# First attention of a four-stage block: the softmax sums of a head group are formed by VectorE additions and one late product with ones

## The chip, the cores and the metric

One core of one Trainium2 chip runs the whole program. The metric is device time in microseconds (us), the median of repeated executions. Engines are named as in the profile: PE is TensorE (PEld its weight loads), DVE is VectorE, ACT is ScalarE, POOL is GpSimd, SP issues most DMAs.

## The reference, cut to what matters

Four residual stages run one after the other on x of shape 4 x 512 x 512: an attention, a feed-forward with ternary weights, a selective scan, and a second attention with a mixture of experts. Only the first attention is touched by the change:

```
q, k, v = heads of (x @ W_qkv.T), 16 heads of 32; q and k rotated, then RMS-normalized
scores = (q . k) / sqrt(32), causal mask
attn   = softmax(scores);   out = (attn @ v) @ W_o.T;   x = x + out
```

The kernel takes exp of the scores without subtracting a maximum, zeroes the masked part, multiplies the weights with v, and divides by the sum of the weights over keys.

## The kernel before, in words

Everything is float32 in this stage. The four batches b are taken one by one. `attend(b, between)` (line 332) works on transposed scores: keys lie on partitions, queries on the free axis. Heads go in four groups g of four heads (HG = 4), keys in four tiles j of 128. Because of the mask, tile j needs only the queries from 128*j on, so it is w = 512 - 128*j wide: 512, 384, 256, 128. The 16 pairs (g, j) are the steps m = 4g + j.

- `scores(g, j)` (line 340) makes four products on PE, one for each head, each with 32 rows (line 346), into two PSUM pairs `sc`; ACT takes exp in two halves into the SBUF tile `pt` (line 351); POOL zeroes the masked corner in the first 128 columns (affine_select, line 352).
- `weigh(g, j)` (line 357) makes eight products on PE (line 364): four with v into the PSUM bank `av`, four with a matrix of ones into the bank `sm`. Each uses 32 columns of the array, one column strip for each head. After j = 3, DVE takes the reciprocal of `sm` (line 372) and multiplies `av` with it (line 373) into `oT`.
- A float32 product shows as two records in the profile, so a set of four products is "x8".

In step m the order on PE is: scores of m, then the parts listed in `between[m]`, then weigh of m - 1. The parts are the projections of the next batch (`project`, line 268: 12 of them, in m = 0 and m = 5 to 15), the output projection of the previous batch (`back`, line 324, in m = 1 to 4), the scaling of q and k (`scale_heads`, line 295, on DVE, in m = 9 and 14), transposes (`turn_heads`, line 317, m = 12 and 13), and small pieces of preparing the ternary weights (`next_job`, line 208: a DMA of `q_w`, then ACT or DVE work). Batch 0 has no `back`, so its steps 1 to 4 have no part; batch 3 has no projections, so its steps 0 and 5 to 16 have no PE part but a tiny one. After the steps come two `turn_heads` and, for the first two batches, the norm of batch b + 2 and `turn_in` (line 262: DVE makes a `row`, two buffers; PE transposes it).

PE's order is the program's, written out by hand (`manual_schedule`, line 387). The order on DVE, ACT and POOL is chosen at build time by a planner that has its own durations; on the chip each of these queues is strictly in that order. A later operation that is ready does not pass one that waits.

Buffers that matter: `pt` has two buffers, so exp of step m writes the one that step m - 2 used. PSUM has eight banks: two pairs for `sc` and four single banks (`bank`, line 67) shared by `av`, `sm`, the projections `pq` and `y`, and the transposes `tp`. `r` has two buffers. The pool `wbig` (line 148) has two buffers of 24 KB a partition for wqkv, w1 and later w3.

Of the kernel before, what the change touches and what calls it, by code (L numbers as in the profile page):

```python
# [11 lines left out]
F32 = mybir.dt.float32  # L12
I32 = mybir.dt.int32
F32R = mybir.dt.float32r
AF = mybir.ActivationFunctionType
ALU = mybir.AluOpType
# [3 lines left out]
P = 128  # L20
B, T, C = 4, 512, 512
NT = T // P
NK = C // P
H, D = 16, 32
NG = H * D // P
HG = P // D
HID = 1365
# [19 lines left out]
def block_kernel(ctx: ExitStack, tc: tile.TileContext, a: dict, out: bass.AP):  # L47
    nc = tc.nc
# [33 lines left out]
    ones = const.tile([P, P], F32, tag="ones", name="ones")  # L82
# [62 lines left out]


    first = ExitStack()
    wbig = first.enter_context(tc.tile_pool(name="wbig", bufs=2, side="right"))


    with tc.tile_pool(name="a_w", bufs=1) as aw, tc.tile_pool(name="a_1", bufs=1) as a1, tc.tile_pool(
        name="a_2", bufs=2
    ) as a2:
        wqkv = wbig.tile([P, NK, 3 * C], F32, tag="wbig", name="wqkv")
        src = by_rows(a["wqkvT"])
# [35 lines left out]
        HW = (HID + 1) // 2  # L191
        parts = {}

        def place(name):
            return wbig.tile([P, NK, HID], F32R, tag="wbig", name=name)

# [45 lines left out]
            scales[name] = ternary_scale(a1, parts[name], name)  # L244

        scales = {}
        w1 = place("w1")

# [66 lines left out]
        def turn_heads(b, t):  # L317
            flat = heads[b][:, t].rearrange("p h d -> p (h d)")
            for s in range(2):
                transpose_into(  # L320
                    turned_qk[b][:, s * NG : (s + 1) * NG, :], flat[:, s * C : (s + 1) * C], t * P
                )
# [9 lines left out]
        def attend(b, between):  # L332

            qkT, v = turned_qk[b], values[b]
            oT = outs[b] = a1.tile([P, NK, T], F32, tag="oT", name="oT")
            weights, sums = {}, {}

            def scores(g, j):  # L340
                w = T - j * P
                pt = weights[g, j] = a2.tile([P, HG, T], F32, tag="pt", name="pt")
                both = [pair("sc") for _ in range(2)]
                for i in range(HG):
                    rows = slice(i * D, (i + 1) * D)
                    nc.tensor.matmul(  # L346
                        both[i // 2][:, i % 2, :w], qkT[rows, NG + g, j * P : (j + 1) * P],
                        qkT[rows, g, j * P :], start=True, stop=True,
                    )
                for i, sc in enumerate(both):  # L350
                    nc.scalar.activation(pt[:, 2 * i : 2 * i + 2, :w], sc[:, :, :w], AF.Exp, scale=SCALE)  # L351
                nc.gpsimd.affine_select(  # L352
                    out=pt[:, :, 0:P], in_=pt[:, :, 0:P], compare_op=ALU.is_ge, fill=0.0,
                    base=0, pattern=[[0, HG], [1, P]], channel_multiplier=-1,
                )

            def weigh(g, j):
                if j == 0:
                    sums[g] = bank("av"), bank("sm")
                pt = weights.pop((g, j))  # L360
                for s, dst in enumerate(sums[g]):
                    for i in range(HG):
                        h = g * HG + i
                        nc.tensor.matmul(
                            dst[i * D : (i + 1) * D, j * P :],
                            ones[:, :D] if s else v[:, j, h * D : (h + 1) * D],
                            pt[:, i, : T - j * P], start=j == 0, stop=j == NT - 1,
                        )
                if j == NT - 1:
                    av, sm = sums.pop(g)  # L370
                    r = a2.tile([P, T], F32, tag="r", name="r")
                    nc.vector.reciprocal(r, sm)
                    nc.vector.tensor_tensor(oT[:, g, :], av, r, ALU.mult)

            steps = [(g, j) for g in range(NG) for j in range(NT)]
            for m in range(len(steps) + 1):
                if m < len(steps):
                    scores(*steps[m])
                for part in between.get(m, ()):
                    part()  # L380
                if m > 0:
                    weigh(*steps[m - 1])

        def do(f, *args):
            return lambda: f(*args)

        with tc.manual_schedule(engines={mybir.EngineType.PE}):

            norm(0, 2)
            for i in range(2):  # L390
                turn_in(0, i)
                for t in (2 * i, 2 * i + 1):
                    project(0, t, 0)
                    project(0, t, 1)
                scale_heads(0, i)
            for i in range(2):
                project(0, 2 * i, 2)
                project(0, 2 * i + 1, 2)
                turn_heads(0, 2 * i)
                turn_heads(0, 2 * i + 1)  # L400
            norm(1)
            turn_in(1, 0)
            turn_in(1, 1)
            w3 = None

            for n in range(2 * NK):
                measure("w1", n)
            at_step = {(0, 1 + 2 * n): n for n in range(2 * NK)}
            scale_at = {(1, 0): "w1", (2, 10): "w2", (3, 0): "w3"}
            for n in range(2 * NK):  # L410
                at_step[1, 1 + 2 * n] = len(jobs)
                quantize(lambda: w1, "w1", n)
                at_step[1, 2 + 2 * n] = len(jobs)
                measure_down(n)
            for n in range(2 * NK):
                if n + 2 * NK < NF:
                    at_step[2, 1 + 2 * n] = len(jobs)
                    measure_down(n + 2 * NK)
                at_step[2, 2 + 2 * n] = len(jobs)
                measure("w3", n)  # L420
            for n in range(2 * NK):
                at_step[3, 1 + 2 * n] = len(jobs)
                quantize(lambda: w3, "w3", n)
            fetch_piece()
            fetch_piece()
            w3 = None
            for b in range(B):
                between = {m: [] for m in range(18)}
                if b > 0:
                    for t in range(NT):  # L430
                        between[1 + t].append(do(back, b - 1, t))
                if b + 1 < B:
                    n = b + 1
                    order = [(0, 0), (0, 1), (1, 0), (1, 1), (0, 2), (2, 0), (2, 1), (1, 2)]
                    order += [(3, 0), (3, 1), (2, 2), (3, 2)]
                    for m, (t, s) in zip([0] + list(range(5, 16)), order):
                        between[m].append(do(project, n, t, s))
                    between[9].append(do(scale_heads, n, 0))
                    between[12].append(do(turn_heads, n, 0))
                    between[13].append(do(turn_heads, n, 1))  # L440
                    between[14].append(do(scale_heads, n, 1))

                for m in range(17):
                    if (b, m) in scale_at:
                        between[m].append(do(find_scale, scale_at[b, m]))
                    if (b, m) in at_step:
                        between[m].append(do(next_job, at_step[b, m]))
                if b == B - 1:
                    first_mv = const.tile([P, NT, 2], F32, tag="mv", name="mv")
                    for t in range(NT):  # L450
                        between[9].append(do(statistics, a1, xs[0], t, first_mv))
                attend(b, between)
                if b + 1 < B:
                    turn_heads(b + 1, 2)
                    turn_heads(b + 1, 3)
                if b + 2 < B:
                    norm(b + 2)
                    turn_in(b + 2, 0)
                    turn_in(b + 2, 1)
                if b + 2 == B:  # L460
                    w3 = place("w3")
            for t in range(NT):
                back(B - 1, t)

# [131 lines left out]
    with tc.tile_pool(name="b_s", bufs=1) as bs, tc.tile_pool(name="b_1", bufs=1) as b1, tc.tile_pool(  # L596
        name="b_2", bufs=2
# [78 lines left out]
        with tc.manual_schedule(engines={mybir.EngineType.PE}):  # L676
# [4 lines left out]
            for b in range(B):  # L681
                hT = high_low.pop(b)
                between = prepare(b - 1, bs, half_pair, 2) if b > 0 else iter(())
# [135 lines left out]
    with tc.tile_pool(name="c_f", bufs=2, reuse_waits="tile") as cf, tc.tile_pool(  # L819
        name="c_1", bufs=1  # L820
# [5 lines left out]
        steps = [(b, n, half) for b in range(B) for n in range(NS) for half in range(2)]  # L826
        loaded, scaled, decays, turned, states, weighed, sums = {}, {}, {}, {}, {}, {}, {}
# [72 lines left out]
        between = prepare(B - 1, cp, bank, 4)  # L900
# [127 lines left out]
    with tc.tile_pool(name="d_1", bufs=1) as d1, tc.tile_pool(name="d_2", bufs=2) as d2, tc.tile_pool(  # L1028
        name="d_3", bufs=3
# [65 lines left out]
        probs, turned_probs, sums, wides, inverses, averages, outs = {}, {}, {}, {}, {}, {}, {}  # L1095
# [79 lines left out]
        with tc.manual_schedule(engines={mybir.EngineType.PE}):  # L1175
# [5 lines left out]
            for m in range(n + 3):  # L1181
                b, at = divmod(m, each)
# [35 lines left out]
    with tc.tile_pool(name="e_1", bufs=1, reuse_waits="tile") as e1, tc.tile_pool(  # L1218
        name="e_2", bufs=2, reuse_waits="tile"
# [55 lines left out]
        total = e1.tile([P, NR], F32, tag="total", name="total")  # L1275
# [15 lines left out]
        place = e1.tile([P, NR, TT], F32, tag="place", name="place")  # L1291
# [247 lines left out]
```

## Time and profile before

| | |
|---|---|
| median of 3 runs | 1933.17 us (1933.12 to 1936.76) |
| profiled execution: its own time | 1941.33 us |
| its span on the core | 1939.6 us |
| mean granted TensorE clock | 0.967 |
| PE busy | 1764.7 us (91%) |
| DVE, ACT, POOL busy | 1143.7 (59%), 946.0 (49%), 580.8 (30%) |
| first attention, first to last score | 63.5 to 412.9 us |

A row of the group view reads: line, engine, operation, what it writes <- what it reads, shapes, count | busy us, mean ns of one | idle time of the engine just before, and what ended it. A row of the timeline reads: start, us, engine, line, operation, count [idle before <- releaser]. Busy times on PE are modelled and overlap a little at the ends; the distance between two starts is the better measure of what one set of products costs.

### The profile page before, as it was taken

To read this page: it belongs to the slowest core of one execution; us is meant where nothing else is said; L and a number is where in the kernel's file an instruction comes from. 1 tells how busy PE (TensorE), PEld (TensorE's weight loads), DVE (VectorE), ACT (ScalarE), POOL (GpSimd) and SP (SyncE) were. 2 spreads that over 40 slices of the span, in tenths; PEclk is the share of its full clock that TensorE was granted. 3 is DMA by queue.
4 is the path that set the end of the run, shared out by engine and by line. 5 is a ranking of instruction groups with operands and counts; after the bars stand their busy time and mean duration, and the time that the engine had idled before them with its cause. 6 is when DMAs were issued, how large, how long until landed. Compare 5 with 4: busy or idle time off the path is not lost. (4 is left out here: it accounts for less than half of the span.)

```text
span 1939.6 us, 26716 instructions
## 1 busy us (share of the span) xinstructions
PE 1764.7 (91%) x9970; PEld 1063.5 (55%) x9970; DVE 1143.7 (59%) x1849; ACT 946.0 (49%) x1945; POOL 580.8 (30%) x391
## 2 busy tenths in 40 slices
PE   7999999989999996977888788999999989999998
PEld 3433343437666664766776655555555554544544
DVE  6456435666454545898999985566574663422222
ACT  2433433332242434978999955556675662111111
POOL 2221212120202020966999850000001000144441
PEclk9999999999999998978999987999999999999999
DMA  7003200101000104115131100000001004645445
GB/s 246 8 1 94 75 1 1 44 25 53 1 34 12 44 1 146 40 60 168 53 101 53 50 14 1 1 1 23 1 23 33 23 2 145 223 88 92 87 83 140
DMA packets 67525, 111.09 MB, mean 57 GB/s; under 512 B 7627, under 2 KB 26443, under 8 KB 67349
## 3 DMA queue, kind: packets, MB, share of 16 engines
q1 hardware_dynamic: 58164, 88.02, 13.8%
q0 software_dynamic: 8656, 20.32, 5.8%
q8 instruction: 80, 1.31, 0.3%
q10 hardware_dynamic: 576, 1.05, 0.1%
q14 instruction: 49, 0.39, 0.1%
HBM read 81.18 MB, written 31.33 MB: 58 GB/s over the span
## 5 line engine op out<-in xcount | busy, mean ns | idle before, releaser
L875 POOL TENSOR_TENSOR hc<-h,cb 128x1024 f32<-128x1024 f32 x128 | 303.4, 2415 | 43.5 <-DVE h L864 28.9
L864 DVE TENSOR_TENSOR_SCAN h<-da,bu 128x512 f32<-128x512 f32 x256 | 289.5, 1197 | 19.4 <-ACT da L848 12.2
L856 PE MATMUL bu<-ident,bu 128*128 128x128 f32 x1024 | 163.7, 291 | 48.8 <-DVE h L864 25.0
L271 PE MATMUL pq<-wqkv,hT 128*128 128x512 f32 x384 | 180.9, 619 | 0.7 <-ACT hT L132 0.7
L842 ACT ACTIVATE bu<-dxT,bts 128x512 f32<-128x512 f32 x256 | 164.4, 721 | 4.6 <-DVE x L716 2.8
L856 PEld LDWEIGHTS bu<-ident,bu 128*128 128x128 f32 x1024 | 122.7, 148 | 79.9 <-ACT bu L842 42.9
L848 ACT ACTIVATE da<-delta_l,am 128x511 f32<-128x511 f32 x256 | 164.6, 721 | 3.6 <-DVE h L864 3.6
L1116 ACT ACTIVATE pr<-scd,nm 128x128 f32<-128x128 f32 (+3 forms) x256 | 132.9, 527 | 58.8 <-DVE nm L1113 56.0
L888 PE MATMUL ys<-ident,hc 128*128 128x128 f32 x1024 | 144.4, 286 | 16.0 <-POOL hc L875 14.0
L653 PE MATMUL pg<-hTh,w 128*128 128x512 f32 (+1 forms) x352 | 148.6, 422 | 4.1 <-DVE sil L659 2.9
L653 PE MATMUL pg<-hTl,w 128*128 128x512 f32 (+1 forms) x352 | 141.5, 402 | 0.2 <-DVE hTl L641 0.2
L1418 PE MATMUL pgr<-wgu,gTe 128*128 x304 | 137.1, 593 | 0.0
L888 PEld LDWEIGHTS ys<-ident,hc 128*128 128x128 f32 x1024 | 121.6, 148 | 26.7 <-POOL hc L875 23.4
L351 ACT ACTIVATE pt<-sc 128x1024 f32<-128x1024 f32 (+3 forms) x128 | 84.1, 697 | 84.2 <-PE sc L346 81.7
L271 PEld LDWEIGHTS pq<-wqkv,hT 128*128 128x128 f32 x384 | 72.0, 196 | 94.7 <-issue 86.2
L1105 PE MATMUL scd<-qkTd 32*128 32x512 f32 (+3 forms) x512 | 108.3, 504 | 12.9 <-ACT pr L1116 11.9
L102 POOL TENSOR_TENSOR ri_ln<-ri_ln,minus_half 128x4 f32<-128x4 f32 (+1 forms) x17 | 16.9, 993 | 319.0 <-DVE ri_ln L101 314.5
L1113 DVE TENSOR_REDUCE nm<-scd 128x2 f32<-128x256 f32 (+3 forms) x128 | 104.0, 813 | 0.0
L1128 PEld LDWEIGHTS tpd<-ident,pr 128*128 128x128 f32 x640 | 70.5, 145 | 60.9 <-issue 41.2
L1128 PE MATMUL tpd<-ident,pr 128*128 128x128 f32 x640 | 102.3, 292 | 0.6 <-ACT pr L1116 0.6
L352 POOL TENSOR_SCALAR_AFFINE_SELECT pt<-pt 128x512 f32<-128x512 f32 x64 | 43.1, 674 | 196.7 <-ACT pt L351 196.7
L1108 DVE TENSOR_TENSOR scd<-scd,neg 128x256 f32<-128x256 f32 x128 | 54.7, 428 | 66.7 <-PE scd L1105 64.9
(263 smaller groups left out, 3107.8 us busy)
## 6 DMA issues: line engine op xcount, KB each, us to landing
cb<-c_rows SPq DMA_DIRECT2D x64, 256.0 KB, 3.1
q_w<-in_w2T SPq DMA_DIRECT2D x20, 256.0 KB, 2.9
deltas<-delta SPq DMA_DIRECT2D x16, 256.0 KB, 2.6
dxs<-st SPq DMA_DIRECT2D x16, 256.0 KB, 2.3
delta_l<-deltas SPq DMA_DIRECT2D x4, 1024.0 KB, 9.5
dxT<-dxs SPq DMA_DIRECT2D x4, 1024.0 KB, 7.1
hrows<-h SPq DMA_DIRECT2D x4, 1024.0 KB, 5.4
acc<-x SPq DMA_DIRECT2D x16, 256.0 KB, 2.0
```

Source lines behind the costliest of these rows:

```text
L271: nc.tensor.matmul(y, inputs_T[b][:, k, t * P : (t + 1) * P], wqkv[:, k, s * C : (s + 1) * C], start=k == 0, stop=k == NK - 1,)
L653: nc.tensor.matmul(pg[:rows, i, :], w[:, k, f * P : f * P + rows], part[:, k, :], start=k + m == 0, stop=k + m == NK,)
L842: nc.scalar.activation(row, dxT[:, t, :], AF.Copy, scale=bts[:, b, t * NS + n : t * NS + n + 1])
L848: nc.scalar.activation(da[:, k, 1:], delta[:, k, 1:], AF.Exp, scale=am[:, k, n : n + 1])
L856: nc.tensor.transpose(bu[i][:, t * P : (t + 1) * P], scaled[b, n][t][:, k * P : (k + 1) * P], ident)
L864: nc.vector.tensor_tensor_scan(h[:, i, :], decays[b, n][:, 2 * half + i, :], bu, 0.0, ALU.mult, ALU.add)
L875: nc.gpsimd.tensor_tensor(hc, states.pop((b, n, half)), weighed[b, n].unsqueeze(1).to_broadcast([P, 2, T]), ALU.mult)
L888: nc.tensor.matmul(sums[b][t][:, k * P : (k + 1) * P], hc[:, i, t * P : (t + 1) * P], ident, is_transpose=True, start=n == 0 and k == 0, s ...
L1105: nc.tensor.matmul(sc[:, i, :w], qkT[at, g, t * P : w], qkT[at, NG + g, :w], start=True, stop=True)
L1116: nc.scalar.activation(pr[:, i, :w], sc[:, i, :w], AF.Exp, bias=nm[:, i : i + 1], accum_out=sums[b, g][:, t, 2 * p + i : 2 * p + i + 1],)
L1128: nc.tensor.transpose(tp[:, j * P : (j + 1) * P], pr[:, i, j * P : (j + 1) * P], ident)
L1418: nc.tensor.matmul(pg, gT[:, k, :], wgu[:, bass.ds(e, 1), k, :].rearrange("p e o -> p (e o)"), start=k == 0, stop=k == NK - 1,)
```

## The change

Each weight tile is kept until DVE has added it to a running sum over the key tiles; PE then multiplies ones with that sum once for each group.

- `pt` becomes two tags with one buffer each: `pta` for even j (512 wide), `ptb` for odd j (384 wide). `r` goes to one buffer. A new tile `pts` (4 heads x 384, one buffer) holds the sum for queries 128 to 511.
- In `scores`, at j = 1 DVE writes pts = pta[128:] + ptb (4 x 384 elements a partition); at j = 2 and 3 it adds the new tile in place (4 x 256, 4 x 128).
- `weigh` makes only the four products with v; at j = 0 also four products with ones for queries 0 to 127.
- A new `total(g)` makes the four products with ones for queries 128 to 511 from `pts`, then the reciprocal and the multiplication. It is called in step 4(g+1) + 1, after the scores and before the parts; for g = 3 it is returned from `attend` and called after the two `turn_heads`.
- w1 gets a tag of its own in `wbig`, whose tags now have one buffer each; wqkv and w3 share the other.

```
-                pt = weights[g, j] = a2.tile([P, HG, T], F32, tag="pt", name="pt")
+                if j % 2 == 0:
+                    pt = a2.tile([P, HG, T], F32, tag="pta", name="pta", bufs=1)
+                else:
+                    pt = a2.tile([P, HG, T - P], F32, tag="ptb", name="ptb", bufs=1)
+                weights[g, j] = pt
...
+                if j == 1:
+                    added[g] = a2.tile([P, HG, T - P], F32, tag="pts", name="pts", bufs=1)
+                    nc.vector.tensor_tensor(added[g], weights[g, 0][:, :, P:], pt[:, :, :w], ALU.add)
+                elif j > 1:
+                    at = added[g][:, :, (j - 1) * P :]
+                    nc.vector.tensor_tensor(at, at, pt[:, :, :w], ALU.add)
+
+            def sum_up(sm, src, at):
+                for i in range(HG):
+                    nc.tensor.matmul(
+                        sm[i * D : (i + 1) * D, at], ones[:, :D], src[:, i, :], start=True, stop=True
+                    )
...
+                av, sm = sums[g]
+                for i in range(HG):
+                    h = g * HG + i
+                    nc.tensor.matmul(
+                        av[i * D : (i + 1) * D, j * P :], v[:, j, h * D : (h + 1) * D],
+                        pt[:, i, : T - j * P], start=j == 0, stop=j == NT - 1,
+                    )
+                if j == 0:
+                    sum_up(sm, pt[:, :, :P], slice(0, P))
+
+            def total(g):
+                av, sm = sums.pop(g)
+                sum_up(sm, added.pop(g), slice(P, T))
+                r = a2.tile([P, T], F32, tag="r", name="r", bufs=1)
+                nc.vector.reciprocal(r, sm)
+                nc.vector.tensor_tensor(oT[:, g, :], av, r, ALU.mult)
...
                     scores(*steps[m])
+                    if m > NT and steps[m][1] == 1:
+                        total(steps[m][0] - 1)
...
+            return lambda: total(NG - 1)
...
-                attend(b, between)
+                finish = attend(b, between)
                 if b + 1 < B:
                     turn_heads(b + 1, 2)
                     turn_heads(b + 1, 3)
+                finish()
```

## The prediction

> **What bounds the kernel now.** The page first. The attention lies in slices 2 to 9 of 40, where PE is at 9 with a few lower slices and DVE at 4 to 6:
>
> ```profile
> PE   7999999989999996977888788999999989999998
> DVE  6456435666454545898999985566574663422222
> ```
>
> Then the windows view from 64 to 418 us, and the groups of that window:
>
> ```profile
> 64.00:418.00 354.00, 334.48 (x2062) 135.49 (x2055) 188.30 (x292) 134.82 (x233) 75.88 (x91) 0.98 0.10 30
> ```
> ```profile
> L372 DVE RECIPROCAL r<-sm 128x512 f32<-128x512 f32 x16 | 53.7, 3355 | 35.4 <-PE sm L364 35.4
> L364 PE MATMUL sm<-pt,ones 128*32 128x128 f32 (+3 forms) x512 | 46.3, 433 | 2.8 <-DVE r L372 2.8
> ```
>
> PE is busy 334.5 of 354 us (94%), DVE 188.3 (53%). Work taken off PE is worth its time here, except where a chain through ACT, POOL and DVE replaces it. The timeline shows what one set of four products costs, by distance of starts (step without a wait):
>
> ```profile
> 190.28 1.07 PE L364 MATMUL av<-pt,v 128*32 128x512 f32 x8
> 191.16 1.04 PE L364 MATMUL sm<-pt,ones 128*32 128x512 f32 x8
> 192.14 0.71 PE L346 MATMUL sc<-qkT 32*128 32x256 f32 x8
> 192.78 3.70 PE L271 MATMUL pq<-wqkv,hT 128*128 128x512 f32 x8
> ```
>
> 512 columns cost 191.16 - 190.28 = 0.88 us; from the like rows 384 cost 0.67, 256 cost 0.46, 128 cost 0.24. Four heads run beside one another: 46.3 us for 512 records of 433 ns.
>
> Third, the waits of the same stretch. PE already stops for the reciprocal, since `av`, `sm`, a projection and the next `av` fill the four single banks:
>
> ```profile
> 105.20 3.35 DVE L372 RECIPROCAL r<-sm 128x512 f32<-128x512 f32 x1
> 106.15 1.07 PE L364 MATMUL av<-pt,v 128*32 128x512 f32 x8
> 108.61 1.06 PE L364 MATMUL sm<-pt,ones 128*32 128x512 f32 x8 [1.39 <-DVE r L372]
> ```
>
> Last, batch 3, groups 1 to 3, where nothing covers the chain (one group every 9.63 us):
>
> ```profile
> 392.83 1.14 PE L346 MATMUL sc<-qkT 32*128 32x512 f32 x8
> 396.16 1.67 ACT L351 ACTIVATE pt<-sc 128x768 f32<-128x768 f32 x2 [0.16 <-PE sc L346]
> 397.95 0.64 POOL L352 TENSOR_SCALAR_AFFINE_SELECT pt<-pt 128x512 f32<-128x512 f32 x1 [1.19 <-ACT pt L351]
> 399.56 1.08 ACT L351 ACTIVATE pt<-sc 128x512 f32<-128x512 f32 x2 [1.73 <-PE sc L346]
> ```
>
> **What it removes.** Per group the products with ones cost 0.88 + 0.67 + 0.46 + 0.24 = 2.25 us. After: 0.24 (j = 0) + 0.67 (total) + about 0.09 for one more change of array shape (384 columns ahead of scores take 0.76, not 0.67) = 1.00. Saved 1.25, times 16 groups: **20 us**, if PE stays the bound everywhere.
>
> **What it adds on DVE.** Additions of 1536, 1024 and 512 elements with both inputs in SBUF. Rows of that kind: 128x1024 (line 312) 1222 ns, 128x512 (line 563) 687 ns; so 1.045 ns an element, and 1536 take 1.76 us. Per group 1.76 + 1.22 + 0.69 = 3.67, in all 58.7 us. DVE goes from 188 to 247 of some 350 us; as a mean it fits. The cost is where its queue stands, in four places.
>
> *(1) Order at j = 1.* When the total of g - 1 has run, the reciprocal (3.36) is ready; the addition of g is ready once the select of (g, 1) is done, and it needs `pts`, which the total frees. The addition stands earlier in the program. Which goes first is the planner's choice, and it decides most of what follows. At 101.7 us the sums were done, yet the planner had put the scaling of heads (line 312, 102.92 to 105.28) ahead of the reciprocal: it takes PE for slower than it is, so both candidates seem ready at once and program order decides. I take the addition first as likelier.
>
> *(2) Banks, in batches 0 to 2.* From the start of the scores of (g, 1): scores 0.86, total until 1.7, projection until 5.3, `av` until 6.2; then `sm` of g needs a fifth bank. Exp ends at 2.55, the select at 3.3 (in the chain of 101.66 us exp began 1.03 later), the addition 5.1, the reciprocal 8.5. PE stands 2.3 to 2.4 us at m = 5 (1.6 in batch 0, where the scores themselves were late). At m = 9 the scaling of heads holds DVE first: reciprocal until 9.4, 3.2 us against today's 1.39, so 1.8 more. At m = 13 the two transposes cover part: 0.9. Sum: 1.6 + 2.4 + 2.4 + 3 x 1.8 + 3 x 0.9 = **14.5 us**. With the reciprocal first it ends at 5.2, and this is 0. Behind the waiting `sm` products stand the next scores and projection.
>
> *(3) Exp behind the addition.* `pta` at j = 2 is free only after the addition of j = 1; before, exp needed only PE's own weigh. Queued behind exp on ACT are copies of v and squares. Where a projection lies between (3.7 us) exp can be some 4 us late unseen. In batch 3 there is none. From 392.83 as zero: select ends 5.76, addition 7.6, exp of j = 2 at 7.65 instead of 6.73; reciprocal until 11.0, the addition of j = 2 until 12.2, which holds exp of the next group (natural 11.3). Period about 11.1 instead of 9.63: the 1.25 is lost and 1.5 paid, 3 x 2.75 = **8.3 us**. With the reciprocal first: addition until 10.1, exp 3.4 late, period 12.65, 3 x 4.25 = 12.8. Batch 0, group 0, is uncovered too, without a reciprocal: **1 us**.
>
> *(4) After the steps.* The last total comes behind two `turn_heads`, about 3.3 us later than today's reciprocal, whereas `turn_in` needs DVE at once:
>
> ```profile
> 145.99 3.36 DVE L372 RECIPROCAL r<-sm 128x512 f32<-128x512 f32 x1 [4.30 <-PE sm L364]
> 149.26 0.52 DVE L122 TENSOR_SCALAR row<-x,mv,ri_ln 128x512 f32<-128x512 f32 x1
> ```
>
> The third row is made right as the reciprocal ends, and PE takes it at 149.93. Moved by 3.3 while PE moves by 0.8, PE waits 2.5, in batches 0 and 1: **5 us**. In batch 3 the last addition and total come ahead of the final reciprocal: **0.9**. The scaling of heads at m = 14 has 4 us to spare; the additions and the later reciprocal use it up; between 0 and 3 us over three batches, I take 0.
>
> The buffers of w1 and w3 and `r` with one buffer: zero; users and order are the same, and both users of `r` are on DVE. No DMA is moved.
>
> **Two rules weighed.** The select takes 634 ns, but 1451 at 104.33, while DVE ran line 312, two SBUF inputs. The Trainium skill, "SBUF — State Buffer", section "SBUF: two separate sides", says why: such a DVE operation and a GpSimd operation take turns on a shared port pair, held for the whole instruction. It speaks against 48 additions of this kind. An addition follows its own select; the next one comes a step later, so I take 0. If each of the 16 long ones met a select for 0.8 us, that would be 13 us of POOL delay, most behind projections; 2 us on PE is the bound.
>
> PE idle: "TensorE: Matmul & The Clock Gate", Part 1, has the clock halved after an idle window of about 3.4 us. Here 2.82 us sufficed:
>
> ```profile
> 181.58 2.56 PE L346 MATMUL sc<-qkT 32*128 32x384 f32 x8 [2.83 <-ACT pt L351]
> 184.07 6.28 PE L271 MATMUL pq<-wqkv,hT 128*128 128x512 f32 x8
> ```
>
> These two took 4.3 us more than the usual 0.9 and 3.7, and the granted clock was 0.57 from 185 to 190. The measurement decides. My gaps are 2.4 us or less, so the sum takes 0; the other end is 4.3 for each group of batch 3 and each long bank wait.
>
> **The sum.** -20 + 14.5 + 8.3 + 1 + 5 + 0.9 = +9.7 us. Against the profiled execution (1941.3 us, 8 above the median, its clock low after the gaps just shown) 1951; on the median of 1933.2, **1943 us**.
>
> **Rivals.**
> - *Reciprocal first everywhere* (0.14): -20 + 12.8 + 1 + 5 + 0.9 = -0.3, **1933 us**. For it: it is ready 0.8 us earlier in batch 3.
> - *Faster* (0.20): reciprocal first behind projections, addition first in batch 3, half of the row wait: -20 + 8.3 + 1 + 2.5 + 0.9 = -7.3, **1926 us**. For it: DVE has 47% idle. Against it: one planner, one rule, two answers.
> - *Slower still* (0.16): my sum, and gaps near 2.8 us halve the clock, or additions stand behind quantize steps that wait for `q_w` (waits up to 3.0 us in batch 1): two such events, +8, **1951 us**. It starts where a gap passes some 2.5 us.
> - The likeliest, addition first (0.50): 1943.
>
> About 0.2% (4 us) is what a measurement can tell from no change. Slower: 0.50 + 0.16; same 0.14; faster 0.20. The range, 1924 to 1952, runs from the faster case to just past the slower.
>
> **What would show it.** Products of `sm` fall from 512 to 256 records, about 20 us busy; DVE gains 48 additions of 1.76, 1.22 and 0.69. PE waits "sm <- DVE r" grow from 2.8 to some 15 us or more if the addition goes first; batch 3's groups take 11.1 us. If those waits stay near 3 and batch 3 takes 12.6, the reciprocal went first. I am wrong if exp of j = 2 never waits for DVE, or if PE shows no wait for `row` after batches 0 and 1.

## The result and the profile after

The changed kernel takes **1959.1 us** (median of 4 runs, 1954.8 to 1964.1) against 1934.0 before (4 runs): a ratio of 1.0128, 95% interval 1.0101 to 1.0155. It is slower by 25 us, where 10 were forecast, and lies above the range of 1924 to 1952. Its profiled execution took 1964.1 us, with a span of 1962.4.

The slices of the profile's page, to be held against those of before. PE's row stands at 8 in slices 2, 4 and 5, which were 9, and DVE's row is fuller by one or two in slices 2 to 8. The last row is the granted clock in tenths: within the attention it is below 9 in slices 2 (49 to 98 us) and 9 (392 to 441), where the attention begins and ends.

```profile
PE   7898899979998998877888788999999989999998
DVE  6567656767545444798999985556574773422222
PEclk9899999989998998898899987999999999999999
```

The whole stage, from the first score to the first transpose of the feed-forward, in the windows view: before, then after. The columns are the length, each engine's busy time and records, and at the end the granted clock, DMA share and GB/s.

```profile
63.47:428.64 365.17, 345.65 (x2087) 140.41 (x2087) 198.13 (x316) 135.35 (x234) 77.66 (x92) 0.98 0.10 29
```
```profile
63.09:452.89 389.80, 347.94 (x1832) 138.91 (x1832) 255.34 (x364) 136.74 (x234) 84.55 (x92) 0.93 0.09 27
```

The stage grew by 24.6 us, the whole loss. PE has 255 records fewer and is yet busy 2.3 us longer. In these traces the granted clock is either full or half, and half for whole windows of 3.41 us: 4 such windows lie in the stage before, 17 in the stage after. So each length can be split into three: idle (length less busy), clock loss (half of the time that PE is busy inside these slow windows), and the rest, which is PE's work at full clock. Before: 19.5 + 6.8 + 338.8. After: 41.9 + 27.2 + 320.8. So **work fell by 18.1, idle rose by 22.3 and clock loss by 20.3**. Batch by batch, from first score to first score, the stage takes 100.0, 113.5, 97.5 and 78.9 us, where it took 88.0, 111.2, 96.5 and 69.5: batches 0 and 3 carry 21.4 of the 24.6.

The groups view of 64 to 430 us after the change, with shapes kept apart:

```profile
L394 DVE RECIPROCAL r<-sm 128x512 f32<-128x512 f32 x15 | 50.3, 3353 | 24.0 <-PE sm L372 24.0
L365 DVE TENSOR_TENSOR pts<-pta,ptb 128x1536 f32<-128x1536 f32 x16 | 27.3, 1709 | 1.5 <-POOL ptb L358 1.5
...
L357 ACT ACTIVATE pta<-sc 128x512 f32<-128x512 f32 x30 | 16.4, 593 | 54.0 <-DVE pts L365 31.4 <-PE sc L352 22.7
...
L372 PE MATMUL sm<-pta,ones 128*32 128x128 f32 x128 | 6.6, 276 | 6.5 <-DVE r L394 6.5
```

The additions cost what was forecast (1.71 us the long one). The third row is the new wait: ACT stands 31.4 us ahead of exp of j = 2, for the long addition. PE's wait for the reciprocal is 6.5 us, not 15: the planner had put the **reciprocal first**. The timeline of group 1 in batch 0 (DVE and PE rows) shows the order and what it does:

```profile
111.66 3.35 DVE L394 RECIPROCAL r<-sm 128x512 f32<-128x512 f32 x1
...
114.93 1.69 DVE L365 TENSOR_TENSOR pts<-pta,ptb 128x1536 f32<-128x1536 f32 x1
115.06 0.43 PE L372 MATMUL sm<-pta,ones 128*32 128x128 f32 x8 [1.93 <-DVE r L394]
...
116.54 0.67 DVE L395 TENSOR_TENSOR oT<-av,r 128x512 f32<-128x512 f32 x1
...
117.26 6.65 PE L271 MATMUL pq<-wqkv,hT 128*128 128x512 f32 x8 [1.14 <-DVE oT L395]
```

Reciprocal, long addition, multiplication: the multiplication, which frees the `av` bank, stands 1.7 us behind the addition, and the next projection waits 1.14 us more for that bank. Then the projection itself takes 6.65 us in place of 3.70. The windows view of 117 to 124 us says why: the granted clock is 0.56.

```profile
117.00:124.00 7.00, 6.74 (x12) 2.68 (x16) 3.38 (x6) 1.42 (x3) 2.96 (x2) 0.56 0.00 0
```

Batch 3, group 1 to 2, in the timeline:

```profile
399.37 3.36 DVE L394 RECIPROCAL r<-sm 128x512 f32<-128x512 f32 x1 [1.34 <-PE sm L372]
...
402.65 1.70 DVE L365 TENSOR_TENSOR pts<-pta,ptb 128x1536 f32<-128x1536 f32 x1
404.26 0.68 DVE L395 TENSOR_TENSOR oT<-av,r 128x512 f32<-128x512 f32 x1
404.44 1.09 ACT L357 ACTIVATE pta<-sc 128x512 f32<-128x512 f32 x2 [4.37 <-DVE pts L365]
...
405.08 0.98 PE L352 MATMUL sc<-qkT 32*128 32x128 f32 x8 [3.28 <-ACT pta L357]
...
407.10 2.09 PE L352 MATMUL sc<-qkT 32*128 32x512 f32 x8
```

Exp starts as the addition ends; PE stands 3.28 us; and the next scores, which wait for nothing, take 2.09 us instead of 1.14. The following group begins at 420.64, so the last group but one takes 13.54 us. The period before was 9.63.

### The profile page after: what moved, and what is told of

Read it like the earlier page. It is cut to its first block, busy times and chain, and to the rows that moved or that the text cites. A ratio compares the mean times of both kernels' runs of the same rounds, so it can differ in the third digit from the quotient of the medians.

```text
span 1962.4 us, 26261 instructions
## 1 busy us (share of the span) xinstructions
PE 1764.3 (90%) x9714; PEld 1059.4 (54%) x9714; DVE 1200.0 (61%) x1897; ACT 947.9 (48%) x1945; POOL 587.5 (30%) x391
## 3 DMA queue, kind: packets, MB, share of 16 engines
q0 software_dynamic: 8656, 20.32, 5.9%
q8 instruction: 78, 1.28, 0.3%
## 5 line engine op out<-in xcount | busy, mean ns | idle before, releaser
L271 PE MATMUL pq<-wqkv,hT 128*128 128x512 f32 x384 | 189.2, 642 | 6.3 <-DVE oT L395 4.7
L914 PEld LDWEIGHTS ys<-ident,hc 128*128 128x128 f32 x1024 | 120.2, 147 | 23.8 <-POOL hc L901 20.5
L1131 PE MATMUL scd<-qkTd 32*128 32x512 f32 (+3 forms) x512 | 108.3, 504 | 13.2 <-ACT pr L1142 12.2
L1451 DVE SCALAR_TENSOR_TENSOR hidr<-pgr,silr 128x256 f32<-128x256 f32 x38 | 16.1, 425 | 130.0 <-ACT silr L1449 130.0
L685 DVE SCALAR_TENSOR_TENSOR sil<-pg,sc_w,sil 128x512 f32<-128x512 f32 (+1 forms) x44 | 32.9, 749 | 91.9 <-ACT sil L684 91.9
```

Of the source, the lines that this page charges most:

```text
L271: nc.tensor.matmul(y, inputs_T[b][:, k, t * P : (t + 1) * P], wqkv[:, k, s * C : (s + 1) * C], start=k == 0, stop=k == NK - 1,)
L914: nc.tensor.matmul(sums[b][t][:, k * P : (k + 1) * P], hc[:, i, t * P : (t + 1) * P], ident, is_transpose=True, start=n == 0 and k == 0, s ...
L1131: nc.tensor.matmul(sc[:, i, :w], qkT[at, g, t * P : w], qkT[at, NG + g, :w], start=True, stop=True)
```

## The experiments

The table has every kernel that ran, with the ratio to the kernel before on the same chip, and the stage of its profiled execution split as above. Work, idle and clock loss are PE's, in us; "slow" counts the windows of 3.41 us at half clock. Six of them (after, no_adds, finish_early, total_early, pool_adds, addition_first) make the same set of products, and their work comes out between 318.9 and 322.1: the split is good to some 3 us, and is read only for differences larger than that.

| kernel | median us | ratio (95%) | stage | work | idle | clock loss | slow |
|---|---|---|---|---|---|---|---|
| before | 1934.0 | 1 | 365.2 | 338.8 | 19.5 | 6.8 | 4 |
| after | 1959.1 | 1.0128 (1.0101 to 1.0155) | 389.8 | 320.8 | 41.9 | 27.2 | 17 |
| e1_no_adds | 1934.6 | 1.0002 (0.9992 to 1.0011) | 362.3 | 320.7 | 28.2 | 13.3 | 8 |
| e2_adds_alone | 1948.8 | 1.0069 (1.0050 to 1.0088) | 381.9 | 341.3 | 27.4 | 13.2 | 8 |
| e4_fill | 1950.9 | 1.0079 (1.0061 to 1.0097) | 378.7 | 335.8 | 30.2 | 12.6 | 8 |
| e5_finish_early | 1954.2 | 1.0083 (1.0058 to 1.0109) | 383.5 | 321.6 | 40.4 | 21.5 | 14 |
| e6_total_early | 1952.8 | 1.0090 (1.0073 to 1.0106) | 377.3 | 322.1 | 36.3 | 18.9 | 12 |
| e8_pool_adds | 1961.0 | 1.0123 (1.0101 to 1.0144) | 390.7 | 318.9 | 42.4 | 29.5 | 20 |
| e9_plain_uncovered | 1937.0 | 1.0006 (0.9997 to 1.0015) | 364.9 | 325.2 | 30.2 | 9.5 | 6 |
| e10_best | 1931.2 | 0.9976 (0.9964 to 0.9989) | 365.8 | 324.3 | 32.6 | 8.9 | 6 |
| e11_best_dve | 1935.5 | 0.9997 (0.9982 to 1.0012) | 363.5 | 327.1 | 28.0 | 8.4 | 5 |
| e12_addition_first | 1974.0 | 1.0196 (1.0171 to 1.0220) | 402.4 | 320.1 | 50.9 | 31.4 | 22 |

**The two halves alone.** e1 keeps the change on PE and leaves out the additions; the late product reads a tile of constants.

```
                 if j == 1:
-                    added[g] = a2.tile(...)
-                    nc.vector.tensor_tensor(added[g], weights[g, 0][:, :, P:], pt[:, :, :w], ALU.add)
-                elif j > 1:
-                    ...
+                    added[g] = still
```

> Leaves out the 48 additions: the late product with ones reads a constant tile of the same size, so the sums are not those of the weights; PE's products and the place of the total are as in the changed kernel. Theory (the loss is DVE's queue: exp and PSUM banks behind the addition and the reciprocal, and the halved clock after the gaps): PE's saving of 20 us is real, and only the late last reciprocal (waits for row after batches 0 and 1, some 8 us with the clock) stays, so about 1922 us. Rival (the saving on PE is not there, because the extra change of array shape and the late total eat it): 1934 us or more.

Measured 1934.6, no change: a miss for the theory, and the side of the rival. The work did fall by 18.1 us, but idle rose by 8.7 and clock loss by 6.5. The late total is not free even without additions: PE waits 8.0 us for the reciprocal (2.8 before) and 6.2 us for `row` (0.7 before). So the gain is all but spent before the first addition is paid for.

e2 keeps all products and the reciprocal as they were, and makes the additions, which nobody reads.

```
-                if j == 0:
-                    sum_up(sm, pt[:, :, :P], slice(0, P))
+                for i in range(HG):
+                    nc.tensor.matmul(sm[i * D : (i + 1) * D, j * P :], ones[:, :D],
+                        pt[:, i, : T - j * P], start=j == 0, stop=j == NT - 1)
+                if j == NT - 1:
+                    total(g)
...
```

> The additions and the new tiles alone: all sixteen products of a group and the reciprocal stay where they were before, and nobody reads the running sum. Theory (it is the order reciprocal, then addition, that costs): here the reciprocal starts a step earlier and is over before the addition is ready, so exp of j = 2 is only about 1 us late in batch 3: 1936 to 1942 us. Rival (58.7 us of additional DVE work, and the port shared with GpSimd, cost by themselves): 1950 us or more.

Measured 1948.8, between the two: the additions alone cost 14 us, and the late total alone (e1) nothing. Together they cost 25, so some 11 us come only where the two meet, with the reciprocal and the long addition next to each other in DVE's queue. Batch 3's last period is 11.2 us against 9.63, and a place came up that nobody had named. In batch 2 (DVE and PE rows of its timeline):

```profile
331.34 1.23 DVE L368 TENSOR_TENSOR pts<-pts,pta 128x1024 f32<-128x1024 f32 x1 [1.06 <-POOL pta L358]
332.48 0.75 DVE L283 TENSOR_TENSOR rot<-pq,sin 128x256 f32<-128x256 f32 x2
333.14 0.68 DVE L287 TENSOR_TENSOR qk<-pq,cos 128x512 f32<-128x512 f32 x1
...
333.97 6.62 PE L271 MATMUL pq<-wqkv,hT 128*128 128x512 f32 x8 [2.71 <-DVE qk L287]
```

An addition waits for its select; the rotation that frees a projection's bank stands behind it in DVE's queue; PE waits 2.71 us and then runs its projection at nearly half speed. This group takes 31.1 us instead of 24.1.

**The clock.** e4 is the changed kernel with useless products put where PE stood: in batch 3 and in batch 0's first group at j = 1, and at one step of batches 0 to 2.

```
+                for _ in range(again(g, j)):
+                    if j == 1:
+                        sum_up(sm, pt, slice(P, T))
+                    else:
+                        ...  # four more products with v, start=True, stop=True
```

> The changed kernel with useless products ahead of the products with v, written to a bank that is written again later: four sets of 384 columns at j = 1 in groups 1 to 3 of batch 3, three in group 0 of batch 0, two sets of 512 at j = 0 of group 2 in batches 0 to 2. They add no dependency on DVE and fill the gaps. Theory (about half of the loss is the halved clock after gaps of 2 to 3 us): 1944 to 1950 us, granted clock back to 1.00 in batch 3. Rival (only the waits count; the slow products are something else): 1959 us or some us more.

Measured 1950.9, just past the theory's range. PE does some 15 us more work (21 sets: 15 of 0.67 us and 6 of 0.88; the split gives 15.0) and the program is 8 us *faster*: idle fell by 11.6, less than what was added, and clock loss by 14.6, with 8 slow windows for 17. So what came back on balance was the clock's. The cure is partial: in batch 3 gaps of 0.70 and 0.64 us remain, with waits for the second half of exp inside the two sets of scores that end them (the set at 400.04 spans 1.83 us for the usual 0.93), and slow products still follow (PE rows of its timeline; 0.85 and 1.04 us are usual for the last two):

```profile
400.04 1.83 PE L352 MATMUL sc<-qkT 32*128 32x384 f32 x8 [0.64 <-ACT pta L357]
401.80 1.29 PE L372 MATMUL sm<-pts,ones 128*32 128x384 f32 x8
402.85 1.95 PE L398 MATMUL av<-pta,v 128*32 128x512 f32 x8
```

**The late total.** e5 calls the last total of a batch ahead of the two `turn_heads`.

```
-                if b + 1 < B:
-                    turn_heads(b + 1, 2)
-                    turn_heads(b + 1, 3)
                 finish()
+                if b + 1 < B:
+                    ...
```

> The changed kernel with the last total of a batch ahead of the two transposes of heads instead of behind them. Theory: the row of the next batch is made in time, as before the change; the waits for row (6.2 us in the changed kernel) and the slow products behind them go: 1948 to 1954 us. Rival (the wait only moves to the transposes, since the total then waits for the addition of j = 3): 1957 to 1961 us.

Measured 1954.2, at the theory's upper end; the interval overlaps that of the changed kernel, so the 5 us are not clear of the noise. The wait for `row` is at its 0.7 us of before, as the theory had it. But much of it only moved, as the rival had it: the total now waits 3.0 us for the addition of j = 3, and the wait for the reciprocal grew from 6.5 to 9.3. Idle fell by 1.5 us in all; the stage is 6.3 us shorter, most of it clock (14 slow windows for 17).

e6 makes every total right behind its group's last product with v, where the kernel before had its reciprocal. That is one set of scores earlier than the change.

```
-                    if m > NT and steps[m][1] == 1:
-                        total(steps[m][0] - 1)
...
                     weigh(*steps[m - 1])
+                    if m % NT == 0:
+                        total(m // NT - 1)
```

> The changed kernel with the total of a group moved up by about one step: right behind the group's last product with v, in the same step, and for the last group too. Theory: the reciprocal is over before the next group's long addition is ready, so exp of j = 2 waits little, the banks come free in time, and the last reciprocal is no later than before; PE may wait about 1 us a group for the addition of j = 3 where nothing covers it: 1918 to 1932 us. Rival (DVE's load as such): still 1950 us or more.

Measured 1952.8, the rival's side; my theory that lateness was the main cost fell here. The order on DVE became reciprocal, multiplication, addition, and the period of batch 3's group 2 is still 12.5 us, for exp of j = 2 still waits 3.5 us for the long addition.

**Which engine adds.** e8 has GpSimd make the additions (`nc.vector.tensor_tensor` to `nc.gpsimd.tensor_tensor`, both places).

> The changed kernel with the 48 additions on GpSimd, in its own queue right behind the selects. From its rope addition (512 elements, 1.28 us) the long one should take about 3.6 us. Theory (DVE's queue is what costs: reciprocal, addition and multiplication behind one another): the waits of PE for the reciprocal and for oT (6.5 and 4.8 us) fall to some 3 us together, while exp of j = 2 in batch 3 is about as late as in the changed kernel: 1942 to 1952 us. Rival (the latency of the additions ahead of exp is what costs, on whichever engine): 1957 us or more.

Measured 1961.0, no better: the rival. DVE is free of the additions, and PE's wait for the multiplication falls from 4.8 to 0.8 us; but the wait for the reciprocal grows from 6.5 to 9.0, and groups 1 and 2 of batch 3 take 15.2 and 13.5 us. The timeline of group 1 (POOL, ACT and PE rows):

```profile
402.45 3.42 POOL L365 TENSOR_TENSOR pts<-pta,ptb 128x1536 f32<-128x1536 f32 x1
...
405.91 1.08 ACT L357 ACTIVATE pta<-sc 128x512 f32<-128x512 f32 x2 [4.30 <-POOL pts L365]
...
406.56 0.98 PE L352 MATMUL sc<-qkT 32*128 32x128 f32 x8 [3.28 <-ACT pta L357]
```

The addition starts earlier, as no reciprocal is ahead of it, and takes twice as long: the same 3.28 us on PE. (In group 2 PE waits only 0.47 us there, for its products run slow: the granted clock is 0.51 from 408.41 to 418.76 us.) What counts is the time until `pta` is free, not whose queue it passes.

**Which groups lose.** e9 gives the four groups that no projection covers (batch 0's first, batch 3's last three) their 16 products and no additions back.

```
+            def plain(g):
+                return b == B - 1 and g > 0 or b == 0 and g == 0
...
-                if j == 1:
+                if plain(g):
+                    pass
+                elif j == 1:
...
-                if j == 0:
+                if plain(g):
+                    ...  # the products with ones as before
+                elif j == 0:
```

> The changed kernel, but the four groups with no projection between (group 0 of batch 0, groups 1 to 3 of batch 3) sum by sixteen products as before and make no additions. Theory (these four carry about 3.9 us each in batch 3 and some 9 us around group 0 of batch 0, clock included): 1938 to 1944 us. Rival (the covered batches carry most): 1952 us or more.

Measured 1937.0, not to be told from before and a little below the theory's range: 4 of 16 groups carried nearly the whole loss (1.22 of 1.28%). The other twelve save some 14 us of work (338.8 to 325.2) and give it back, by waits on PE: for `row` 6.7 us, for the reciprocal 7.9, for the multiplication 4.8. Here the same pair of gaps is seen with and without a price (PE rows, batch 0 and batch 2):

```profile
107.84 0.43 PE L377 MATMUL sm<-pta,ones 128*32 128x128 f32 x8 [1.92 <-DVE r L408]
110.04 3.70 PE L271 MATMUL pq<-wqkv,hT 128*128 128x512 f32 x8 [1.14 <-DVE oT L409]
...
320.67 0.43 PE L377 MATMUL sm<-pta,ones 128*32 128x128 f32 x8 [1.92 <-DVE r L408]
322.88 5.25 PE L271 MATMUL pq<-wqkv,hT 128*128 128x512 f32 x8 [1.14 <-DVE oT L409]
```

e10 adds to e9 what e6 and e8 do: the total early, the additions on GpSimd.

> Three edits together: the four uncovered groups plain, the additions of the other twelve on GpSimd, and the total of a group right behind its last product with v (so the last total is not late either). Theory: twelve groups keep most of the 1.25 us that they save on PE, and no new wait is left: 1917 to 1930 us. Rival (what the chip gains on PE it loses again to waits for exp, banks and clock): 1934 us or more.

Measured 1931.2, just past the theory's range: 0.24% faster than before (interval 0.11% to 0.36%), the only version that beats both kernels. Where its 4.6 us lie, one profile can't say: its stage is as long as that of before, and the part behind the stage, whose code is the same, took between 1500.5 and 1511.0 us over all these profiles.

e11 is e10 with the additions on VectorE.

> The four uncovered groups keep 16 products; the other twelve are summed with the total right behind their last v product, as in the last version, but with the additions on VectorE. Theory (in covered groups the engine that adds hardly matters; what counts is that no chain stands bare): 1928 to 1937 us, a ratio of 0.997 to 1.001, and bank waits (products with ones behind the reciprocal) of some 8 us as with GpSimd. Rival (additions on VectorE hold the rotation and the multiplication that free the banks, which is why the plain-uncovered version with VectorE kept nothing): 1939 us or more, and new PE waits for the multiplication or for the rotated heads of 5 us or more.

Measured 1935.5, in the theory's range. PE waits 0.9 us for rotated heads and has no new wait for the multiplication, where the rival had 5 or more. Its interval overlaps that of e10, so which engine adds in covered groups stays untold.

**The order that I had taken as likelier.** e12 is the changed kernel with one copied column that forces the addition ahead of the reciprocal.

```
                 r = a2.tile([P, T], F32, tag="r", name="r", bufs=1)
+                if g + 1 in added:
+                    nc.vector.tensor_copy(r[:, :1], added[g + 1][:, 0, :1])
                 nc.vector.reciprocal(r, sm)
```

> The changed kernel, with one added copy of a column of the sum into the reciprocal's tile, which forces the long addition ahead of the reciprocal of the group before, the order that the prediction took as likelier. By the prediction's sum (waits for the reciprocal 14.5 us, a group of batch 3 every 11.1 us, no clock loss): 1943 us, ratio 1.005. Theory (gaps of 1 to 2.4 us already bring slow products, so the clock term is missing in either order): 1953 to 1970 us, with 15 us or more of bank waits, a batch 3 group of 11 to 12.5 us and a clock loss of 20 us or more up to the end of the stage.

Measured 1974.0, above even the theory. Groups 1 and 2 of batch 3 take 13.0 and 12.0 us. PE's wait for the reciprocal, in the groups view of the stage, is 23.3 us:

```profile
L372 PE MATMUL sm<-pta,ones 128*32 128x128 f32 x128 | 7.5, 311 | 23.3 <-DVE r L396 23.3
```

A third buffer for the weight tiles, which would take exp's wait for the addition away, was not tried: there is no room for it in SBUF.

## Why the prediction was wrong

**The step that failed is the clock term: "My gaps are 2.4 us or less, so the sum takes 0."** It was 20 us. Put the prediction's own waits beside the runs:

- For the order that the planner chose, reciprocal first, the rival's waits were 12.8 + 1 + 5 + 0.9 = 19.7 us. Idle rose by 22.3.
- For the order that I had taken, they were 14.5 + 8.3 + 1 + 5 + 0.9 = 29.7 us. In e12 idle rose by 31.4.

Both sums hold within 3 us, and the work saved, 20, was measured as 18.1. That the sums hold is in part luck. In the changed kernel the waits of scores for exp grew by 8.5 us (10.0 to 18.5) where 12.8 + 1 were forecast, and the banks took 8.5 where 0 was. In e12 the reciprocal's wait grew by 20.5 us, not 14.5, and the wait of the scores for exp hardly at all. The times are nevertheless 26 us above 1933 and 31 above 1943: clock loss rose by 20.3 us in the one and by 24.6 in the other. I had taken the one row at hand, a slow group behind a gap of 2.83 us, as a threshold; it was only an example. After the change a pair of gaps, 1.93 and 1.14 us with 1.1 us of work between, is followed by a clock of 0.56. The trace of before held a counterexample too (PE rows, batch 3):

```profile
361.42 1.83 PE L346 MATMUL sc<-qkT 32*128 32x384 f32 x8 [0.86 <-ACT pt L351]
363.18 5.40 PE L327 MATMUL y<-wo,oT 128*128 128x512 f32 x8
```

A gap of 0.86 us, and 0.9 us more inside the set of scores that ends it, were enough to make a set of products of 3.70 us take 5.40; the clock is 0.50 from 363.37 to 366.78. The other end that I had named, 4.3 us "for each group of batch 3 and each long bank wait", makes 30 over the seven such places (three groups, four bank waits): too much, but nearer than 0.

**When a gap costs** can be read from the traces. Cut the stage of each of the twelve into the windows in which its clock changes, 3.41 us each. Of 1182 windows at full clock, 50 had PE busy for less than 45%, and the next window was at half clock every time. In 969 PE was busy for 80% or more, and the next was at half clock never. Between the two it was 31 of 163. So what counts is not the length of one gap but how much of one window is idle: 1.9 us of 3.41 (55%) was always too much. A slow stretch lasts on in the same way: all 25 windows at half clock with PE busy under 80% were followed by another. Here are the two like pairs of gaps of e9 in their windows (after the length comes PE's busy time; the third number from the end is the clock):

```profile
104.17:107.58 3.41, 1.75 (x10) 0.16 (x8) 3.41 (x2) 0.00 (x0) 0.00 (x0) 1.00 0.00 0
107.58:110.99 3.41, 2.02 (x18) 0.96 (x19) 3.41 (x6) 1.08 (x2) 0.35 (x1) 1.00 0.00 0
110.99:114.41 3.42, 3.42 (x15) 1.11 (x13) 1.54 (x3) 0.63 (x1) 2.61 (x2) 1.00 0.00 0
319.21:322.62 3.41, 1.07 (x16) 0.47 (x16) 3.41 (x3) 0.29 (x1) 0.00 (x0) 1.00 0.00 0
322.62:326.03 3.41, 3.15 (x4) 1.51 (x5) 2.69 (x5) 0.79 (x2) 2.49 (x2) 0.50 0.00 0
```

In batch 0 a boundary falls between the gaps, PE is busy 1.75 and 2.02 us in the two windows, and the clock stays full. In batch 2 most of both lies in one window, PE is busy 1.07 us, and the next window is at half clock. The Trainium skill, "TensorE: Matmul & The Clock Gate", Part 1, describes the clock as set by activity over a free-running window of about 3.4 us; the 3.41 us and the two outcomes of one pair agree with it, and so does the grid of windows, which lies differently against the program in every trace. Priced by its rule of an idle window, the changed kernel's gaps would have cost nothing, as in the prediction; the windows above show that a window need not be wholly idle.

**The order** was wrong too: the planner put the reciprocal first. By itself this would have brought the time down, to the 1933 of that rival; with the clock it didn't. The "slower still" case had the right mechanism, a halved clock, but put it at two events of some 4 us each and beyond gaps of 2.5 us: 8 us of the 20.

**Banks, with the reciprocal first: "this is 0."** It was 8.5 us: 3.7 more for the reciprocal and 4.8 for the multiplication behind the long addition (four waits of 1.14 and one of 0.20). I had followed the reciprocal, which frees one bank, and not the multiplication, which frees the other one.

**Batch 3** with the reciprocal first was to take 12.65 us a group; groups 1 and 2 took 14.56 and 13.54 (11.70 and 9.63 before). The chain (addition ends, exp, scores) is as described; the rest goes with the clock, here from 407 to 411 us in the windows view:

```profile
407.00:411.00 4.00, 3.48 (x24) 1.02 (x20) 1.18 (x2) 1.78 (x2) 0.98 (x1) 0.63 0.00 0
```

With the clock at 0.63 the scores at 407.10 end 0.95 us late (2.09 for 1.14), and the exp that opens the next chain starts behind them: that is about the 0.9 by which 13.54 exceeds 12.65. With the addition first a group was to take 11.1; in e12 group 2 took 11.99, with its idle time as before (0.74 us for 0.73): there too the rest goes with the clock, 0.51 from 420 to 430 us.

**Batch 0, group 0, "1 us":** it took 14.43 us for 12.60, with gaps of 1.54 and 1.63, and behind them the clock is 0.57 from 77 to 91 us, a loss of 6 us. The covered group that follows took 23.86 us for 20.32 (18.60 in e9, where the first group is as before). It was the largest miss in one place: an uncovered group slows the covered one behind it.

**The row wait** (5 us forecast) was 5.5 more than before (6.2 for 0.7): right; but e5, which removed it, got other waits for most of it. The durations of the long and short additions (1.71 and 0.69 us; the middle one took 1.36 for 1.22) were right as well, and the new buffers cost nothing that shows, for e1 has them too. So was the small effect of the shared port pair: one select took 1.36 us beside an addition, at 406.62, and nothing on PE waited for it.

**What stays open** is what decides in the windows with PE busy for 45 to 80%. The profile counts a set of scores that waits inside for the second half of exp as busy, so these shares are too high by an unknown amount. No run moved a gap on purpose against the windows; that they decide is read from where the gaps fell.

## What to carry to other kernels

Price idle time on PE at up to twice its length when PE is otherwise full: over these runs clock loss rose by 0.2 to 1.0 us for each us of added idle, and by 0.5 to 1.0 in all that lost over 0.5%. Don't compare single gaps with a limit; add up the idle time that can fall into one window of 3.41 us. Before moving sums off PE, look for the stretches that no other product covers and leave those as they are; here a quarter of the groups carried over nine tenths of the loss. And where a buffer is shared, follow every operation that must end before it is free, and every one behind it in the same queue: the multiplication and the rotation mattered here as much as the reciprocal.

## What the runs showed of the hardware

- Useless products can make a program faster: some 15 us of them took 8 us off (e4).
- The granted clock is full or half, and half for whole windows of 3.41 us (4 to 22 of them in the stage of the twelve traces). Every window at full clock with PE idle for more than 55% of it was followed by one at half clock (50 of 50), none with PE idle for 20% or less (0 of 969).
- Two short gaps add up: 1.93 and 1.14 us are followed by a clock of 0.56 over 7 us (after).
- An addition of 128x1536 with two inputs in SBUF takes 1.71 us on DVE and 3.42 on POOL (the latter a rough span, but the exp that waited for it began 3.46 us after its start).
